# A four-layer block stack in fp32: two multiplications of the weights' fp4 rounding on GpSimd, another end for filler matmuls, and other due times

## The chip, the cores and the metric

The kernel runs on one core of a Trainium2 chip. The metric is the device time of one execution in microseconds (us); the time of a kernel is the median of several executions. Times of single instructions and waits are from one profiled execution.

## The reference, cut to what matters

The input x is 8 sequences of 1024 rows of 256 numbers (fp32). Four blocks follow, each added to what went in:

```python
x = x + attn0(layernorm(x))   # linear attention with running sums, then an inner FFN with GELU
x = x + ffn0(layernorm(x))    # relu(x @ w1 + b1) @ w2 + b2, 256 -> 1024 -> 256
x = x + attn1(layernorm(x))   # softmax attention, one head of 256
x = x + ffn1(layernorm(x))    # the FFN with fp4 rounding, 256 -> 704 -> 256
```

The change touches the rounding in the last block. It works on blocks of 16 numbers:

```python
def fp4_quant_dequant(x):
    xb = x.reshape(shape[:-1] + (shape[-1] // BLOCK, BLOCK))
    scale = jnp.max(jnp.abs(xb), axis=-1, keepdims=True) / 6.0
    scale = jnp.maximum(scale, jnp.float32(1e-12))
    xn = xb / scale
    idx = jnp.searchsorted(_MID, jnp.abs(xn))
    q = _GRID[idx] * jnp.sign(xn) * scale
    return q.reshape(shape)
```

Both sides of each product are rounded: the rows, for every row, and the weights w_gate, w_up (704 x 256) and w_down (256 x 704), once.

## The kernel before, in words

**Work.** The 8192 rows are cut into 64 chunks of 128 rows; four chunks are a group, two groups a sequence, so there are 16 groups. A group passes through the linear attention (linear_group, linear_span, linear_chunk), through the two dense FFNs (dense, with norms_1 after the first and norms_2 after the second), and then each chunk through the softmax attention and the fp4 FFN (soft_chunk). Different groups are in different stages at the same time, so that the stages share TensorE. A matmul of fp32 is two passes in the trace.

**Order.** Each stage is a Python generator that yields what its next instruction needs: an engine, tiles that must be written, free PSUM banks, a condition, a due time. Plan.run (L375) holds a small reckoning of when each engine and tile is free (Plan.took, L221) and always goes on with the part that can start soonest; among equals it prefers TensorE, and then the earliest due time. The instructions of each engine are pinned in the order in which they were issued: this order is fixed when the program is built, and the chip follows it. The queues of VectorE (DVE), ScalarE (ACT), GpSimd (POOL), TensorE (PE) and SyncE (SP, which issues the DMAs) are each in order.

**Due times.** T (L31) has a value for each kind of step, and EARLY (L78) other values for stages of the planner's time: below 130, 260, 400 and 2150, and after that. A value with a digit (lin2, weights0) is for one group alone. Other values are margins: ripe_* for how early something may be asked for, back and ahead for how far engines may run apart, shy for how much later ScalarE may be than VectorE and still get a layernorm's last step (layernorm, L705), gate0 and gate1 for the stage at which a group may begin.

**Fillers.** Where the planner finds that TensorE would wait over 1.6 us, it issues matmuls of the identity with itself into a free bank (fill, L1842); nobody reads these products. They run until 0.6 us ahead of the time at which the planner expects the next step.

**Transposes.** flip (L734) transposes a tile for the next product: on TensorE with a copy by ScalarE, if the planner finds no other step ready for TensorE, and otherwise by a copy on GpSimd (cut), a transposing DMA (spun) and a copy by ScalarE.

**The fp4 rounding** (fp4, L797) is a chain: VectorE takes the largest magnitude of each block (x_amax), the scale (x_s) and its reciprocal (x_r), multiplies the tile by x_r and a constant, ScalarE squares the scaled tile into q_c (bf16), VectorE rounds in two steps with q_c, and multiplies by x_s. fp4_weights (L838) runs the chain over 18 pieces of the three weights (tiles w_raw, at most 128 x 256), transposes each on TensorE, and copies it to wgT, wuT or wdT. When the last is done, "fp4" is added to the set weights. soft_chunk (L1688) runs the same chain over n (128 x 256) and hid (128 x 704) of each chunk, and asks for "fp4" in weights before the gate product (L1778).

All instructions are issued by one helper, so the profile has L422 for nearly all of them, and they are told apart by their tiles: half and hidden are the inputs of the two dense products with w_in and w_out, n2T and qT of the softmax scores, probT and vt of the attention product, xqT with wgT and wuT of gate and up, hqT with wdT of the last product, ident of fillers and of transposes.

Of the kernel before, what the change touches and what calls it, by code (L numbers as in the profile page):

```python
# [14 lines left out]
ALU = mybir.AluOpType  # L15
AX = mybir.AxisListType

P = 128
# [19 lines left out]
    gate1=1, by_act=1,  # L38
# [38 lines left out]

EARLY = [  # L78
    (130.0, dict(
        prods=0.359, pair=0.052, weighted=0.011, sums2=0.405, scores=0.861, turn_k=0.81,  # L80
        xo=0.296, step=0.131, dense=0.051, soft=2.551, soft1=0.323, soft2=0.706, fp4_over=5.754,
        weights=0.044, ripe_t=1.058, ripe_v=0.456, ripe_s=0.249, ripe_g=0.541, ripe_d=9.276,
        lin3=0.344, dense1=-0.003, weights0=-1.017, weights1=0.043,
    )),
    (260.0, dict(
        span=-0.064, prods=0.185, sums=-0.114, chunk=0.702, scores=0.785, dense=-0.085,
        soft=3.213, soft1=0.121, weights=-0.008, ripe_s=0.838, back=0.505, lin=-0.259,
        lin0=-0.325, norm0=-0.157, norm1=-0.26, weights0=-0.379, weights1=0.063, gate1=3.5,
    )),
    (400.0, dict(  # L90
        prods=-0.044, turn_k=0.82, turn_h=0.707, step=0.103, norm=0.746, soft=3.784, soft3=0.912,
        fp4=2.195, weights=0.078, ripe_d=7.2, ahead=0.839, lin2=-0.414,
    )),
    (2150.0, dict(
        prods=0.106, pair=0.211, sums=0.071, weighted=0.176, chunk=0.596, turn_k=0.801, xo=0.47,
        turn_h=0.706, soft3=1.013, fp4=3.733, fp4_over=6.383, weights=0.169, ripe_d=6.945,
        ahead=0.541, lin1=0.497, lin2=-0.186, lin3=-0.528, dense0=-0.017, dense1=0.151,
        norm0=-0.113, weights0=-0.286, gate1=3,
    )),
    (1000000000.0, dict(  # L100
        lin3=0.54, ripe_d=5.647, lin1=0.423, dense1=-0.052, scores=0.713, xo=0.287, chunk=0.609,
        shy=0.81, back=0.523, sums2=0.353,
    )),
]

# [18 lines left out]
class Plan:  # L124
# [206 lines left out]
    def dve(self, *tiles, **kw):  # L331
        return self.need("vector", tiles, **kw)
# [42 lines left out]
    def run(self):  # L375
        while self.parts:
            now = self.free.get("tensor", 0.0)
            best = None
            for part in self.parts:
                t = self.ready(part[1])  # L380
                if t is None:
                    continue
                stays = self.tiled and part[1].tiled
                queue = part[1].queue
                wait = max(max(t) - now - (0.3 if stays or part[2] < 0.0 else 0.0), 0.0)
                urgent = part[2] < 0.0
                unripe = 0.0 if urgent else max(t[1] + self.times[RIPE[queue]] - now, 0.0)
                key = wait, unripe, queue == "tensor", not stays, part[2]
                if best is None or key < best[0]:
                    best = key, part, max(t)  # L390
            assert best is not None, "every part waits for another"
            until = max(now, best[2])
            if until - self.ran > 1.6 and best[1][1].queue == "tensor" and self.fill is not None:
                if (self.banks_free(best[1][1].banks + 1) or 0.0) <= self.ran + 0.4:
                    self.fill(until - 0.6)
                    self.ran = until - 0.6
            if best[0][0] > 0.0 or best[1][1].queue == "tensor":
                self.free["tensor"] = max(now, best[2])
# [42 lines left out]
def block_stack_kernel(ctx: ExitStack, tc: tile.TileContext, a: dict, out: bass.AP):  # L441
# [20 lines left out]
    plan = Plan(tc, tc.nc)  # L462
# [328 lines left out]
    def blocks(t, width):  # L791
        return t[:, :width].rearrange("p (b e) -> p b e", e=QB)

    def wide(v, rows, nb):
        return v.unsqueeze(2).to_broadcast([rows, nb, QB])

    def fp4(src, width, rows=P, factor=1.0):  # L797

        nb = width // QB
        src = src[:rows, :width]
        amax = small([P, INTER // QB], "x_amax", 2)[:rows, :nb]
        nc.vector.tensor_reduce(
            amax, blocks(src, width), AX.X, ALU.max, apply_absolute_value=True  # L810
        )
        sc = small([P, INTER // QB], "x_s", 4)[:rows, :nb]
        nc.vector.tensor_scalar(sc, amax, factor / 6.0, 1e-12, ALU.mult, ALU.max)
        rc = small([P, INTER // QB], "x_r", 3)[:rows, :nb]
        nc.vector.reciprocal(rc, sc)
        yield dve(rc)
        nc.vector.scalar_tensor_tensor(
            blocks(src, width),
            blocks(src, width),
            -factor * (1.0 - 2.0**-23),  # L820
            wide(rc, rows, nb),
            ALU.mult,
            ALU.mult,
        )
# [12 lines left out]

    def fp4_weights():  # L838
        pieces = []
        for name, dstT in (("L1_ffn_w_gate", wgT), ("L1_ffn_w_up", wuT)):  # L840
            for r0, rows in INTER_TILES:
                turns = [(dstT[:, k, r0 : r0 + rows], k * P, P) for k in range(2)]
                pieces.append((a[name][r0 : r0 + rows, :], turns))
        for n in range(2):
            for c0 in range(0, INTER, D):
                width = min(D, INTER - c0)
                turns = []
                for f0 in range(0, width, P):
                    rows = min(P, width - f0)
                    dst = wdT[:rows, (c0 + f0) // P, n * P : (n + 1) * P]  # L850
                    turns.append((dst, f0, rows))
                pieces.append((a["L1_ffn_w_down"][n * P : (n + 1) * P, c0 : c0 + width], turns))
        raws = {}
        for i, (src, turns) in enumerate(pieces):
            for j in range(i, min(i + 3, len(pieces))):
                if j not in raws:
                    ahead = pieces[j][0]
                    raws[j] = (yield from fresh(
                        "soft",
                        dma(at=times["fp4"] + times["fp4_over"] * i / len(pieces), when=lambda: count["stage"] >= times["stage"]),  # L860
                        "w_raw",
                    ))[
                        : ahead.shape[0], : ahead.shape[1]
                    ]
# [823 lines left out]
    def soft_chunk(cc):  # L1688
# [209 lines left out]
```

## Time and profile before

| what | value |
|---|---|
| median of 3 runs | 2450.55 us (2448.66 to 2452.24) |
| the profiled execution's own time | 2450.4 us |
| its span | 2448.7 us |
| mean granted TensorE clock | 0.999 |
| DMA | 312.74 MB, 128 GB/s on average, 51% of the 16 engines' time |

The span is the time from the first to the last instruction of the profile, and the execution's own time has 1.7 us around it. Busy shares don't say how well an engine is used: matmuls overlap in the pipeline and their ends are modelled, so a busy TensorE may have slack, and fillers count as busy. A group's row has its line, engine, operation and tiles (out<-in), then the count, the busy time in us and the mean length of one in ns, and then the engine's idle time ahead of them and what ended it. A row of the timeline begins with start and length in us; what stands in brackets is idle time before it and what ended that.

### The profile page before, as it was taken

How to read it: one execution, taken by the hardware profiler on the slowest of the kernel's cores; microseconds unless marked ns; L12 is line 12 of the kernel's file. 1: busy time of each engine (PE TensorE's matmuls, PEld its weight loads, DVE VectorE, ACT ScalarE, POOL GpSimd, SP SyncE). 2: the span in 40 equal slices, each digit the busy share in tenths (PEclk: the TensorE clock that was granted, in tenths of full speed). 3: DMA queues.
4: the chain of work that ended last, by engine and by line, in shares of the span. 5: the costliest groups of instructions: out<-in, count | busy, mean ns of one | idle time of the engine just before them, and what ended most of it. 6: DMA issues, size and time to landing. Idle time of an engine off the chain costs nothing.

```text
span 2448.7 us, 47669 instructions
## 1 busy us (share of the span) xinstructions
PE 2419.4 (99%) x16473; PEld 1891.6 (77%) x16473; DVE 1914.3 (78%) x4152; ACT 1387.7 (57%) x2895; POOL 1276.9 (52%) x2258
## 2 busy tenths in 40 slices
PE   8999999999999999999999999999999999999999
PEld 6877777777877777777777777777777777887777
DVE  7778787878779787787877888688886978765887
ACT  5454556565565645656565565655556465555454
POOL 4354556565555656365563655546555474544342
PEclk9999999999999999999999999999999999999999
DMA  3355455564655555546555554556545555545332
GB/s 106 91 150 160 123 151 128 139 146 121 145 135 121 140 139 129 138 115 155 132 122 134 125 150 125 139 131 124 141 127 133 143 118 145 124 126 129 67 83 59
DMA packets 630897, 312.74 MB, mean 128 GB/s; under 512 B 434304, under 2 KB 619136, under 8 KB 630656
## 3 DMA queue, kind: packets, MB, share of 16 engines
q1 hardware_dynamic: 630656, 309.70, 51.3%
q8 instruction: 130, 2.13, 0.4%
q14 instruction: 111, 0.91, 0.1%
HBM read 188.17 MB, written 20.71 MB: 85 GB/s over the span
## 4 chain that ended last, share of the span: by engine, by line
PE 88%; DVE 6%; DMA 2%; POOL 2%; issue 1%; ACT 1%; SPq 0%; DVEq 0%; POOLq 0%; ACTq 0%
PE bank L422 88%; DMA spun<-cut 2%; DVE hid L422 1%; POOL cut L422 1%; DVE prod L422 1%; DVE ln_st L422 1%; DVE n L422 0%; POOL ln_rstd L422 0%; DVE sc L422 0%; DVE mx L422 0%; DVE res L422 0%; DVE u L422 0%; SPq L422 0%; POOL ln_shift L422 0%; DMA w_in<-in_L_attn_W_dram 0%
## 5 line engine op out<-in xcount | busy, mean ns | idle before, releaser
L422 PE MATMUL bank<-half,w_in 128*128 128x256 f32 x2048 | 529.2, 381 | 9.5 <-ACT half L422 6.4
L422 PE MATMUL bank<-w_out,hidden 128*128 128x256 f32 x2048 | 525.6, 383 | 1.5 <-DMA w_out<-in_L_attn_W_dram 1.4
L422 PEld LDWEIGHTS bank<-w_out,hidden 128*128 128x128 f32 x2048 | 377.4, 190 | 105.1 <-issue 45.7
L422 PEld LDWEIGHTS bank<-half,w_in 128*128 128x128 f32 x2048 | 384.5, 190 | 87.9 <-issue 22.4
L422 POOL TENSOR_SCALAR ln_ve<-ln_mv 128x1 f32<-128x1 f32 x384 | 107.1, 279 | 510.6 <-DVE ln_mv L422 489.4
L422 POOL TENSOR_TENSOR ln_rstd<-ln_ve,neghalf 128x1 f32<-128x1 f32 x384 | 251.3, 654 | 32.0
L422 ACT ACTIVATE hidden<-bank,c_L_ffn_b 128x256 f32<-128x256 f32 x256 | 120.8, 472 | 223.8 <-PE bank L422 222.0
L422 PE MATMUL bank<-n2T,qT 128*128 128x512 f32 x512 | 241.5, 594 | 0.0
L422 PE MATMUL bank<-vt,probT 128*128 128x256 f32 x1024 | 231.2, 379 | 0.0
L422 PEld LDWEIGHTS bank<-vt,probT 128*128 128x128 f32 x1024 | 194.2, 190 | 32.9 <-issue 6.9
L422 POOL COPY cut<-n 128x512 uint16<-128x512 uint16 x233 | 175.0, 757 | 79.8 <-DVE n L422 68.4
L422 ACT ACTIVATE hidden<-bank,c_L_attn_b 128x256 f32<-128x256 f32 x256 | 119.7, 469 | 170.8 <-PE bank L422 170.0
L422 POOL COPY cut<-prob 128x512 uint16<-128x512 uint16 x213 | 147.8, 716 | 92.0 <-ACT prob L422 50.4
L422 POOL COPY cut<-hid 128x512 uint16<-128x512 uint16 x172 | 116.4, 694 | 144.3 <-DVE rsum L422 66.3
L422 PE MATMUL bank<-wdT,hqT 128*128 128x256 f32 x768 | 175.9, 379 | 0.0
L422 PE MATMUL bank<-wgT,xqT 128*128 128x352 f32 x512 | 173.8, 462 | 0.5 <-ACT xqT L422 0.5
L422 PE MATMUL bank<-wuT,xqT 128*128 128x352 f32 x512 | 172.3, 459 | 0.0
L422 ACT COPY probT<-spun 128x512 uint16<-128x512 uint16 x250 | 159.6, 674 | 13.3 <-DMA spun<-cut 12.8
L422 PEld LDWEIGHTS bank<-wdT,hqT 128*128 128x128 f32 x768 | 145.6, 190 | 22.7 <-issue 1.9
L422 ACT ACT_TABLE_LOAD x124 | 159.1, 1283 | 4.4 <-PE bank L422 2.2
L422 PEld LDWEIGHTS bank<-n2T,qT 128*128 128x128 f32 x512 | 96.4, 190 | 69.7 <-issue 56.4
L422 PEld LDWEIGHTS bank<-wuT,xqT 128*128 128x128 f32 x512 | 97.3, 190 | 54.2
(272 smaller groups left out, 4831.1 us busy)
## 6 DMA issues: line engine op xcount, KB each, us to landing
w_in<-in_L_attn_W_dram SPq DMA_DIRECT2D x128, 256.0 KB
w_out<-in_L_attn_W_dram SPq DMA_DIRECT2D x128, 256.0 KB
w_in<-in_L_ffn_w_dram SPq DMA_DIRECT2D x128, 256.0 KB
w_out<-in_L_ffn_w_dram SPq DMA_DIRECT2D x128, 256.0 KB
spread<-packed SPq DMA_DIRECT2D x90, 256.0 KB
spun<-cut SPq DMA_TRANSPOSE x768
x<-in_L_attn_inputs_dram SPq DMA_DIRECT2D x64, 128.0 KB
xr<-in_L_attn_inputs_dram SPq DMA_DIRECT2D x64, 128.0 KB
```

The lines of the kernel that those rows point to most:

```text
L422: ins = method(*args, **kw)
```

## The change

Four things:

1. In fp4 a new argument, pooled, moves the two wide multiplications (by x_r with the constant, and by x_s) from VectorE to GpSimd. The constant is multiplied into x_r first, by one small instruction on VectorE. Only fp4_weights asks for it.
2. A burst of fillers ends 1.0 us ahead of the next step's expected time, and not 0.6.
3. soft_chunk waits for the weights' rounding before its second layernorm, and still before its gate product.
4. EARLY has other values in all its stages.

```diff
@@ EARLY
 (130.0, dict(
-        prods=0.359, pair=0.052, weighted=0.011, sums2=0.405, scores=0.861, turn_k=0.81,
-        xo=0.296, step=0.131, dense=0.051, soft=2.551, soft1=0.323, soft2=0.706, fp4_over=5.754,
-        weights=0.044, ripe_t=1.058, ripe_v=0.456, ripe_s=0.249, ripe_g=0.541, ripe_d=9.276,
-        lin3=0.344, dense1=-0.003, weights0=-1.017, weights1=0.043,
+        span=-0.169, prods=0.359, pair=0.034, weighted=0.011, sums2=0.405, scores=0.861,
+        turn_k=0.705, xo=0.464, turn_h=1.351, step=0.131, dense=0.051, norm=0.637, soft=2.551,
+        soft1=0.323, soft2=0.581, fp4=1.292, fp4_over=1.373, weights=0.044, shy=1.271,
+        ripe_t=1.087, ripe_v=0.344, ripe_s=0.249, ripe_g=0.541, lin0=0.017, lin2=-1.332,
+        lin3=0.34, dense1=-0.034, norm0=-0.179, weights0=-0.978, weights1=0.643,
     )),
...
     (2150.0, dict(
-        prods=0.106, pair=0.211, sums=0.071, weighted=0.176, chunk=0.596, turn_k=0.801, xo=0.47,
-        turn_h=0.706, soft3=1.013, fp4=3.733, fp4_over=6.383, weights=0.169, ripe_d=6.945,
-        ahead=0.541, lin1=0.497, lin2=-0.186, lin3=-0.528, dense0=-0.017, dense1=0.151,
-        norm0=-0.113, weights0=-0.286, gate1=3,
+        prods=0.106, pair=0.277, sums=-0.139, weighted=0.176, chunk=0.596, turn_k=0.859, xo=0.47,
+        turn_h=0.706, soft3=1.013, fp4=3.733, fp4_over=6.383, ahead=0.541, lin2=0.062,
+        lin3=0.238, dense0=-0.017, dense1=0.351, norm0=-0.113, norm1=-0.217, weights0=-0.402,
+        gate1=3, weights=0.1,
     )),
...
@@ Plan.run
-                    self.fill(until - 0.6)
-                    self.ran = until - 0.6
+                    self.fill(until - 1.0)
+                    self.ran = until - 1.0
@@ fp4
-    def fp4(src, width, rows=P, factor=1.0):
+    def fp4(src, width, rows=P, factor=1.0, pooled=False):
...
         nc.vector.reciprocal(rc, sc)
-        yield dve(rc)
-        nc.vector.scalar_tensor_tensor(
-            blocks(src, width),
-            blocks(src, width),
-            -factor * (1.0 - 2.0**-23),
-            wide(rc, rows, nb),
-            ALU.mult,
-            ALU.mult,
-        )
+        if pooled:
+            nc.vector.tensor_scalar(rc, rc, -factor * (1.0 - 2.0**-23), None, ALU.mult)
+            yield plan.pool(rc)
+            nc.gpsimd.tensor_tensor(
+                blocks(src, width), blocks(src, width), wide(rc, rows, nb), ALU.mult
+            )
+        else:
+            yield dve(rc)
...
         nc.vector.scalar_tensor_tensor(src, c, k, src, ALU.add, ALU.subtract)
         plan.drop(tile_c)
-        nc.vector.tensor_tensor(
+        if pooled:
+            yield plan.pool(src)
+        (nc.gpsimd if pooled else nc.vector).tensor_tensor(
             blocks(src, width), blocks(src, width), wide(sc, rows, nb), ALU.mult
         )
@@ fp4_weights
-            yield from fp4(raw, width, rows)
+            yield from fp4(raw, width, rows, pooled=True)
@@ soft_chunk
         yield dve(rows)
+        yield dve(when=lambda: "fp4" in weights)
         n = yield from layernorm("soft", rows)
```

Since the order of all engines follows from the due times, the built program differs nearly everywhere in its order, though hardly in what it computes: VectorE has 4148 instructions instead of 4154, GpSimd 2293 instead of 2263, TensorE 8359 matmuls and weight loads instead of 8349.

More of the change, by code (lines that the diff above doesn't have):

```diff
@@ L84 @@
+        soft1=0.323, soft2=0.581, fp4=1.292, fp4_over=1.373, weights=0.044, shy=1.271,
+        ripe_t=1.087, ripe_v=0.344, ripe_s=0.249, ripe_g=0.541, lin0=0.017, lin2=-1.332,
+        lin3=0.34, dense1=-0.034, norm0=-0.179, weights0=-0.978, weights1=0.643,
     )),
     (260.0, dict(
-        span=-0.064, prods=0.185, sums=-0.114, chunk=0.702, scores=0.785, dense=-0.085,
-        soft=3.213, soft1=0.121, weights=-0.008, ripe_s=0.838, back=0.505, lin=-0.259,
-        lin0=-0.325, norm0=-0.157, norm1=-0.26, weights0=-0.379, weights1=0.063, gate1=3.5,
+        span=0.206, prods=0.185, sums=-0.114, chunk=0.75, scores=0.785, dense=-0.085, soft=2.917,
@@ L89 @@
+        soft1=0.121, soft2=1.012, soft3=0.802, fp4=1.6, fp4_over=1.861, weights=0.254,
+        ripe_s=0.807, ripe_g=0.295, ripe_d=6.404, lin=-0.238, lin0=-0.325, lin3=-0.136,
+        norm0=-0.157, norm1=-0.498, weights1=-0.069, shy=0.28,
     )),
     (400.0, dict(
-        prods=-0.044, turn_k=0.82, turn_h=0.707, step=0.103, norm=0.746, soft=3.784, soft3=0.912,
-        fp4=2.195, weights=0.078, ripe_d=7.2, ahead=0.839, lin2=-0.414,
+        prods=-0.044, weighted=0.483, turn_k=0.82, turn_h=0.707, step=0.103, norm=0.746,
@@ L93 @@
+        soft2=0.443, soft3=1.065, fp4=1.6, fp4_over=2.0, weights=-0.335, ripe_s=0.657,
+        ripe_d=7.2, ahead=0.839, lin=-0.054, lin0=-0.32, lin2=-0.414, dense1=-0.304,
+        norm0=-0.074, norm1=-0.125, weights0=-0.121, gate0=3,
     )),
     (2150.0, dict(
-        prods=0.106, pair=0.211, sums=0.071, weighted=0.176, chunk=0.596, turn_k=0.801, xo=0.47,
-        turn_h=0.706, soft3=1.013, fp4=3.733, fp4_over=6.383, weights=0.169, ripe_d=6.945,
-        ahead=0.541, lin1=0.497, lin2=-0.186, lin3=-0.528, dense0=-0.017, dense1=0.151,
@@ L98 @@
-        norm0=-0.113, weights0=-0.286, gate1=3,
+        prods=0.106, pair=0.277, sums=-0.139, weighted=0.176, chunk=0.596, turn_k=0.859, xo=0.47,
+        turn_h=0.706, soft3=1.013, fp4=3.733, fp4_over=6.383, ahead=0.541, lin2=0.062,
+        lin3=0.238, dense0=-0.017, dense1=0.351, norm0=-0.113, norm1=-0.217, weights0=-0.402,
+        gate1=3, weights=0.1,
     )),
     (1000000000.0, dict(
-        lin3=0.54, ripe_d=5.647, lin1=0.423, dense1=-0.052, scores=0.713, xo=0.287, chunk=0.609,
-        shy=0.81, back=0.523, sums2=0.353,
+        lin3=-0.292, ripe_d=5.647, lin1=0.423, dense1=0.111, ripe_g=0.48, xo=0.287, chunk=0.609,
@@ L103 @@
+        shy=1.949, back=0.523, sums2=0.353, prods=0.274, soft=4.117, ripe_s=0.0, sums=-0.155,
+        ahead=0.482, weights=0.091, fp4_over=2.929, lin2=-0.073, soft1=0.477,
     )),
@@ L815, in fp4 @@
         nc.vector.reciprocal(rc, sc)
-        yield dve(rc)
-        nc.vector.scalar_tensor_tensor(
-            blocks(src, width),
-            blocks(src, width),
-            -factor * (1.0 - 2.0**-23),
-            wide(rc, rows, nb),
-            ALU.mult,
-            ALU.mult,
-        )
+        if pooled:
[6 more added lines that the diff above has]
+            yield dve(rc)
+            nc.vector.scalar_tensor_tensor(
+                blocks(src, width),
+                blocks(src, width),
+                -factor * (1.0 - 2.0**-23),
+                wide(rc, rows, nb),
+                ALU.mult,
+                ALU.mult,
+            )
         tile_c = yield from fresh("q_c", act(src))
```

## The prediction

> **What bounds the kernel now.** I read the busy row first, then the chain of waits, then TensorE's groups, its timeline around the fillers, and at last the rows of the operations that move.
>
> ```profile
> PE 2419.4 (99%) x16473; PEld 1891.6 (77%) x16473; DVE 1914.3 (78%) x4152; ACT 1387.7 (57%) x2895; POOL 1276.9 (52%) x2258
> PE 88%; DVE 6%; DMA 2%; POOL 2%; issue 1%; ACT 1%; SPq 0%; DVEq 0%; POOLq 0%; ACTq 0%
> L422 PE MATMUL bank<-ident 128*128 128x128 f32 x282 | 35.5, 285 | 3.1 <-POOL ident masks.py:199 3.1
> ```
>
> TensorE is the bound: busy 99%, and 88% of the chain that ended last. Only 29 us of the 2448.7 are idle, but 282 passes write products that nobody reads (two passes for each filler matmul of the program, so 141 fillers). Starts of neighbouring filler passes lie 112 ns apart, so one filler takes 0.224 us and all take 31.6 us. What can be won is in idle time and fillers, some 60 us, and most of that is the start-up, where no work exists yet.
>
> ```profile
> 320.00:500.00 180.00, 179.62 (x1269) 141.12 (x1268) 142.97 (x315) 103.09 (x217) 100.68 (x175) 1.00 0.55 137
> 1081.00:1375.20 294.20, 293.32 (x1998) 229.13 (x1998) 234.25 (x499) 171.14 (x350) 162.87 (x284) 1.00 0.54 133
> 2415.00:2449.00 34.00, 28.45 (x154) 23.31 (x153) 23.21 (x40) 10.82 (x21) 4.76 (x6) 0.99 0.19 47
> ```
>
> These are busy sums of three stretches (length; then PE, PEld, DVE, ACT, POOL). In the long middle the work repeats every two groups, 294.2 us, with 0.9 us idle in each. From 320 to 2150 us TensorE waits 5.2 us in all: six times for half from ScalarE, 4.8 us together, once 0.4 us for a weight. The middle offers at most this; but if the new order makes a wait there, it is paid about six times. The rest is the first 320 us and the last 34.
>
> ```profile
> 61.08 4.41 PE L422 MATMUL bank<-ident 128*128 128x128 f32 x38
> 101.52 5.97 PE L422 MATMUL bank<-ident 128*128 128x128 f32 x52
> 108.01 0.44 PE L422 MATMUL bank<-ident,h 128*128 128x128 f32 x2 [0.52 <-DVE h L422]
> 213.11 1.13 PE L422 MATMUL bank<-half,w_in 128*128 128x256 f32 x4 [1.83 <-DMA w_in<-in_L_attn_W_dram]
> 2431.07 5.07 PE L422 MATMUL bank<-ident 128*128 128x128 f32 x44
> ```
>
> There are twelve bursts. In eight the next step started within 0.1 us of the last filler; at six of these its input had been written 0.38 to 1.45 us before the start (0.05 where nothing was in the way): the filler held it up. After four a hole followed (0.32 to 1.99 us).
>
> **Fillers, and the end of a burst at 1.0 instead of 0.6 us.** I count them in the order in which the two built programs list their instructions; no time is taken from the planner's own reckoning. 141 become 139, but not in the same places:
> - Up to the second transpose of h before the first dense stage (108.0 us), 98 become 82: 16 x 0.224 = -3.6 us. Of the holes (1.9 us before) the two large ones, 1.11 and 0.68, grow by 0.4 each; the bursts that overshot only stop overshooting. +0.7. **Sum -2.9**; ends -3.6 (no hole grows) and +1.5 (seven holes of a full 1.0).
> - From there to 320 us, 15 become 18: +0.7, and two holes grow by 0.4: **+1.5** (0 to +2). The weights at 203 to 213 us stay late: in the new order of SyncE, too, the next w_in stands behind the four spread transfers.
> - In the middle, where there were none, eight stand ahead of a w_out product: 1.8 us plus a hole of up to 1.0. **+2.3** (0, if they take the place of another wait, to +2.8).
> - At the end 28 become 31, in four bursts instead of two: +0.7. Each hole could be 1.0; the holes in this tail were 0.32 and 1.39, and I add 1.1. **+1.8** (0 to +3.6).
>
> A longer hole could let the clock fall. The row speaks first:
>
> ```profile
> 28.00:32.00 4.00, 2.00 (x22) 1.00 0.11 33
> 32.00:35.00 3.00, 0.98 (x4) 0.50 0.01 3
> 35.00:39.00 4.00, 3.54 (x6) 0.52 0.43 118
> ```
>
> (length, PE busy, granted clock, DMA.) The clock halved at 32 us after 4 us in which TensorE was half busy, and half of the 3.5 us of work at the lower clock, 1.7 us, was lost. The Trainium skill (TensorE: Matmul & The Clock Gate, What's actually happening) lets it fall after about 3.4 us of idleness; by that rule holes of 1.5 us cost nothing, by the row a thin stretch is enough and each new dip costs about 1.7 us. This dip stays in both, since the same steps stand there. I add no second one, and keep 1.7 us for the range.
>
> **Transposes on TensorE** (flip, when the planner finds TensorE idle): 113 matmuls become 125, each two passes of 109 ns. Ten more stand in the first 320 us, where half may lie in idle time (+1.1), six more in the middle, which has no idle time (+1.3), four fewer between 2150 and 2400 (-0.9). **+1.5** (0 to +2.6). The DMA transposes fall from 768 to 762, on a queue off the path.
>
> **The two wide multiplications.**
>
> ```profile
> L422 DVE SCALAR_TENSOR_TENSOR w_raw<-w_raw,x_r x18: 345/416/605, 47.0 to 297.5; 128x256 f32<-128x256 f32 x14, 64x256 f32<-64x256 f32 x2, 128x192 f32<-128x192 f32 x2
> L422 DVE TENSOR_TENSOR w_raw<-w_raw,x_s x18: 357/425/835, 58.5 to 311.7; 128x256 f32<-128x256 f32 x14, 64x256 f32<-64x256 f32 x2, 128x192 f32<-128x192 f32 x2
> L422 DVE TENSOR_SCALAR x_s<-x_amax 128x16 f32<-128x16 f32 x78 | 18.9, 242 | 2.7
> L422 POOL TENSOR_TENSOR res<-n,b_L_attn_bo 128x256 f32<-128x256 f32 x64 | 51.0, 801 | 6.8 <-ACT carry_w L422 4.0 <-DMA b_L_attn_bo<-in_L_attn_bo_dram 2.1 <-ACT ahead L422 0.7
> ```
>
> VectorE loses 18 x (416 + 425 ns) = 15.1 us and gains 18 small multiplications at 242 ns, 4.4 us: 10.8 us less between 45 and 320 us. GpSimd has no such form with a broadcast input; its additions of this shape take 748 to 1011 ns, and I take 801, since it too reads two tiles: 36 x 0.80 = 29 us more on a queue that was half busy. A piece's chain gets 2 x 0.80 - 0.84 + 0.24 = 1.0 us longer and crosses engines four times. This is hidden: by the summed work of TensorE the last transpose of w_raw stands at 257 us (253 before), and the first gate product at 297 in both, so 40 us of other work cover it. Without that cover it would cost some 4 us once.
>
> A rule speaks against this part. The Trainium skill (SBUF — State Buffer, Who interferes with whom) says that a VectorE instruction with two inputs in SBUF is shut out while a GpSimd instruction reads SBUF. By the rows alone VectorE gains the 10.8 us. By the rule it is blocked in some of the new 29 us: it is busy 79% of that stretch, and if half of that has two such inputs, 29 x 0.79 x 0.5 = 11 us are lost again, an estimate. The x_s row, with 835 ns at most against 357 at least, is of a kind that would do so. I take it that little reaches TensorE: in 45 to 320 us it waits only 1.2 us for VectorE openly, and ahead of the second h, which is VectorE's chain, there are 36 fillers where 34 stood. Queued behind a wide multiplication on GpSimd are the layernorm steps (ln_rstd) and the cuts, each up to 0.8 us later, and ScalarE's n waits for these. **+1.0** (-1.2, the open waits gone, to +3).
>
> **The wait for the weights moved ahead of the layernorm** in soft_chunk: the weights' transposes end at 257 us of TensorE's work and the first attention product, after which it stands, at 266. It holds nothing: **0**; were it late, only a chunk's layernorm on VectorE stands behind it.
>
> **Due times in the middle.** Six transposes on TensorE in each two groups before and after; table loads on ScalarE fall from 16 to 14 per two groups (2 x 1.28 us, ScalarE is 57% busy). No wait shows in an order: **0** (-4.8 to +4.8).
>
> **Sum:** -2.9 + 1.5 + 2.3 + 1.8 + 1.5 + 1.0 = +5.2. The profiled execution took 2450.4 us (span 2448.7 and 1.7 around it), within 0.2 of the median 2450.55. **Forecast 2456 us, slower by 0.2%.** All lower ends give 2441, all upper ends with a second dip some 2472.
>
> **Rivals.** (1) Faster: the six waits for half go. For: in the new order two gate and two up products (2.4 us) lie between the transpose of n and the dense product at the step of that kind. Then -4.8, with -3.6 at the start, -1.2 for VectorE, +1.8 middle burst, +0.7 tail, +0.5 transposes: -6.6, 2444 us. Against: these waits only moved in the order, and ScalarE has to copy a second chunk too. (2) No change: the start's gain and half of these waits (-2.4) pay for the rest, with no price on GpSimd and no larger holes at the end: +0.7, 2451 us. (3) Much slower: the new order makes one wait of 2 us in each two groups, at the run of six attention and gate steps with no dense product between: 6 x 2 = +12 on the forecast, 2468 us. Against: the planner places transposes as often as before. That the change does nothing is excluded: the 36 multiplications stand on GpSimd.
>
> **Numbers.** Forecast 0.44, (1) 0.30, (2) 0.13, (3) 0.13. The range 2440 to 2470 leaves out about 2 in 10; the forecast's own is 2452 to 2462. A difference under 0.2% (4.9 us) can't be told from none. Faster: 0.28 + 0.02 = 0.30. Slower: 0.36 of the forecast, 0.01 and 0.13 = 0.50. Within: 0.20.
>
> **What would show it.** Right: filler passes near 278; the transpose of the second h before 108.0 us; a burst near 520 us; more idle time after the last gate product; w_raw on GpSimd near 0.8 us. Wrong: no wait for half left in the middle (rival 1), or a new wait that returns every 294 us (rival 3); a second stretch at half clock; w_raw on GpSimd over 1.0 us with late layernorms.

## The result, and the profile after

The changed kernel takes **2463.08 us** (median of 6 runs, 2460.08 to 2464.39), the kernel before in the same session 2450.33 us. The ratio is **1.0046, 95% interval 1.0036 to 1.0057**: slower by some 11 us, where 2456 (slower) was forecast with a range of 2440 to 2470. The profiled execution took 2464.0 us with a span of 2462.3, 13.6 more than the span before.

The page of the changed kernel (busy time, chain of waits, and the row of the fillers with its count, busy time, mean length, and idle time ahead):

```profile
PE 2426.9 (99%) x16481; PEld 1892.4 (77%) x16481; DVE 1907.2 (77%) x4146; ACT 1366.3 (55%) x2862; POOL 1317.9 (54%) x2288
PE 84%; DVE 10%; ACT 2%; POOL 2%; DMA 1%; issue 1%; SPq 0%; DVEq 0%; POOLq 0%; ACTq 0%
L427 PE MATMUL bank<-ident 128*128 128x128 f32 x278 | 35.2, 284 | 3.1 <-POOL ident masks.py:199 3.1
```

TensorE's idle time (span less busy) rose from 29.3 to 35.4 us, 6.1 more. Its busy time rose by 7.5 though its products are the same and the filler passes fell by 4: part of it is 12 more transposing passes in the trace (185 for 173, 1.3 us at 109 ns). Most of the rest is time at half clock: TensorE was busy for 14.3 us in three stretches at half clock (10.24, 3.41 and 3.41 us long), and before for 4.3 us in one (6.83 us long). Half of the difference, 5.0 us, is an estimate of what this added. VectorE is less busy and GpSimd more, as intended, and the chain has more of VectorE.

The busy sums of four stretches of the changed kernel (length; PE, PEld, DVE, ACT, POOL, each with its count of instructions; granted clock; DMA share and GB/s):

```profile
320.00:500.00 180.00, 179.62 (x1226) 140.24 (x1225) 144.71 (x318) 102.62 (x220) 99.82 (x179) 1.00 0.56 141
500.00:620.00 120.00, 115.92 (x815) 88.87 (x814) 87.14 (x186) 69.31 (x131) 58.37 (x108) 1.00 0.50 124
1085.00:1379.20 294.20, 293.48 (x1998) 228.77 (x1997) 234.25 (x498) 168.81 (x345) 169.12 (x283) 1.00 0.54 133
2428.00:2462.30 34.30, 29.60 (x164) 24.45 (x162) 23.52 (x42) 11.38 (x22) 3.70 (x6) 1.00 0.22 54
```

In the early part, in one stretch of the middle and in the tail the idle time is about that of before; stretches of equal length do not show whether a period has become longer. The stretch that stands out is 500 to 620 us: TensorE is idle for 4.1 us there, where about the same work had 1.1 us of idle time in the kernel before:

```profile
490.00:610.00 120.00, 118.94 (x824) 92.23 (x823) 93.34 (x195) 72.69 (x140) 70.57 (x119) 1.00 0.57 135
```

Busy sums do not add up to a finish time, so I also compared progress. Each product of TensorE, without fillers and transposes, is given its spacing from the traces (112 ns for 128 columns, 216 for 256, 429 for 512; passes of 32 rows a quarter), and the table says how many us later than the kernel before a run has done so much of this work (the columns; 2290 us in all). All kernels of this study stand in it; runs of one order differ by up to 2 or 3 us.

| run | 110 | 200 | 450 | 600 | 1200 | 1800 | 2250 | end |
|---|---|---|---|---|---|---|---|---|
| changed kernel | 0.7 | 0.2 | 1.2 | 6.4 | 7.3 | 9.0 | 13.3 | 13.7 |
| burst_alone | 1.0 | 1.5 | 0.6 | 1.2 | 1.1 | 1.1 | 1.1 | 3.0 |
| pool_alone | 0.0 | 0.5 | -0.5 | -0.5 | -0.3 | -0.1 | -0.1 | 0.0 |
| due_alone | 11.8 | 17.5 | 35.1 | 34.2 | 38.7 | 39.7 | 41.4 | 42.8 |
| after_burst_06 | 1.8 | 5.4 | 6.4 | 11.1 | 12.1 | 13.0 | 14.9 | 16.0 |
| all_due_old | 1.7 | 10.8 | 15.8 | 16.4 | 27.6 | 29.9 | 32.0 | 32.2 |
| new_order_mults_on_vector | 1.8 | 3.5 | 4.4 | 9.8 | 11.2 | 12.7 | 17.3 | 17.7 |
| late_due_old | -0.3 | -0.5 | -0.5 | -1.8 | 2.0 | 11.9 | 12.3 | 13.5 |
| early_due_old | 2.7 | 9.8 | 12.9 | 17.2 | 18.0 | 20.6 | 25.2 | 25.6 |
| one_due_moved | 0.7 | 4.0 | 9.8 | 14.1 | 21.6 | 24.2 | 32.5 | 36.0 |
| one_function_before | -1.1 | -1.0 | -0.7 | -0.8 | -0.8 | -0.4 | -0.4 | -0.4 |
| one_function_after | -1.2 | -0.3 | 0.6 | 2.6 | 3.6 | 5.5 | 8.5 | 8.9 |
| start_filled | -0.3 | 0.4 | 1.4 | 1.9 | 1.8 | 1.9 | 2.5 | 3.9 |

For the changed kernel: about 1 us is lost in the first 450 us of work, 5.0 us at one place between 450 and 500 (542 to 599 us of its trace), a slow drift after that, and 4.3 us between 1800 and 2250.

TensorE's timeline in the changed kernel, at the bursts that the prediction spoke of (start and length in us; in brackets idle time and what ended it):

```profile
23.87 4.18 PE L427 MATMUL bank<-ident 128*128 128x128 f32 x36
30.96 0.48 PE L427 MATMUL bank<-ident,n 128*128 128x128 f32 x1 [2.91 <-ACT n L427]
...
99.06 8.20 PE L427 MATMUL bank<-ident 128*128 128x128 f32 x72
107.11 0.38 PE L427 MATMUL bank<-ident,h 128*128 128x128 f32 x2
...
114.37 0.86 PE L427 MATMUL bank<-prod,hsum 128*32 128x128 f32 x24 [1.48 <-DVE prod L427]
...
564.73 1.95 PE L427 MATMUL bank<-ident 128*128 128x128 f32 x16
```

The second h comes at 107.11 instead of 108.01 us, but TensorE then waits 1.48 us for prod. The hole at 28 us has grown to 2.91 us (0.95 before). The burst in the middle is there, at 564.7 us; it was expected near 520.

Rows of TensorE's waits in the changed kernel (us in all, times, longest):

```profile
PE bank L427 <- ACT half L427: 3.0, 4, 1.8
PE bank L427 <- DVE hid L427: 2.1, 5, 0.4
...
PE bank L427 <- DVE sc L427: 1.5, 5, 0.3
```

The same for half in the kernel before:

```profile
PE bank L422 <- ACT half L422: 6.4, 9, 0.9
```

There hid had 1.4 us in one wait, and sc was not there. So the large waits for half did leave the middle, and two smaller ones came in their place in each period, one for hid and one for sc.

The two multiplications on GpSimd in the changed kernel (count, busy time, mean ns, idle time ahead):

```profile
L427 POOL TENSOR_TENSOR w_raw<-w_raw,x_s 128x256 f32<-128x256 f32 (+2 forms) x18 | 14.1, 784 | 29.8 <-DVE w_raw L427 29.8
L427 POOL TENSOR_TENSOR w_raw<-w_raw,x_r 128x256 f32<-128x256 f32 (+2 forms) x18 | 12.4, 690 | 25.7 <-DVE x_r L427 18.0 <-issue 7.4
```

Their mean is 0.74 us, against the 0.80 taken.

### The profile page after: what moved, and what is told of

Same layout as the page of the kernel before. It is cut to its first block, busy times and chain, and to the rows that moved or that the text cites. A ratio compares the mean times of both kernels' runs of the same rounds, so it can differ in the third digit from the quotient of the medians.

```text
span 2462.3 us, 47584 instructions
## 1 busy us (share of the span) xinstructions
PE 2426.9 (99%) x16481; PEld 1892.4 (77%) x16481; DVE 1907.2 (77%) x4146; ACT 1366.3 (55%) x2862; POOL 1317.9 (54%) x2288
## 4 chain that ended last, share of the span: by engine, by line
PE 84%; DVE 10%; ACT 2%; POOL 2%; DMA 1%; issue 1%; SPq 0%; DVEq 0%; POOLq 0%; ACTq 0%
PE bank L427 84%; DVE prod L427 3%; DVE hid L427 2%; DVE spread L427 1%; DMA spun<-cut 1%; DVE ln_st L427 1%; DVE n L427 1%; ACT L427 1%; POOL ln_rstd L427 0%; DVE x_amax L427 0%; DVE ln_mv L427 0%; DVE u L427 0%; DVE q L427 0%; DVE res L427 0%; POOL cut L427 0%
## 5 line engine op out<-in xcount | busy, mean ns | idle before, releaser
L427 POOL TENSOR_SCALAR ln_ve<-ln_mv 128x1 f32<-128x1 f32 x384 | 119.1, 310 | 573.4 <-DVE ln_mv L427 550.2
L427 POOL TENSOR_TENSOR ln_rstd<-ln_ve,neghalf 128x1 f32<-128x1 f32 x384 | 238.1, 620 | 32.0
```

Of the source, the lines that this page charges most:

```text
L427: ins = method(*args, **kw)
```

## Experiments

### Each part alone

Three theories: the loss lies in the order of instructions that the new due times make (1), in the multiplications on GpSimd (2), or in the earlier end of the bursts and the clock (3). Four kernels, on one chip, where the kernel before took 2452.35 us.

**burst_alone.** The kernel before with the new end of bursts.

```diff
-                    self.fill(until - 0.6)
-                    self.ran = until - 0.6
+                    self.fill(until - 1.0)
+                    self.ran = until - 1.0
```

> The kernel before with bursts ending 1.0 us ahead; the order of everything but the fillers is that of before (121 fillers instead of 141). Theory 1 (the loss lies in the order that the new due times make): 2449 to 2452 us. Theory 2 (the loss lies in the multiplications on GpSimd): the same. Theory 3 (the earlier end of the bursts lets TensorE's clock fall more often or for longer): 2453 to 2456, with more than 7 us at half clock.

Measured: 2453.80 us, ratio 1.0006 (0.9999 to 1.0012). The order of all other instructions is that of before; only the fillers are 121 instead of 141. Twenty fillers less, 4.5 us at 0.224, won nothing: the start is 1.0 us late at 110 us of work. The bare time and the some 14 us at half clock of its trace are what theory 3 gave; but on this chip the kernel before took 2452.35 us, so the difference is 1.5 us, and its interval holds zero.

**after_burst_06.** The changed kernel with the old end of bursts (the same edit, reversed).

> The changed kernel with bursts ending 0.6 us ahead again; same order but for the fillers (159 instead of 139). Theories 1 and 2: 2462 to 2465, no nearer to before. Theory 3: 2457 to 2460, and less than 13 us at half clock.

Measured: 2462.91 us, ratio 1.0051 (1.0038 to 1.0063), the same as with 1.0, and 17.1 us at half clock as there. Theory 3 falls: of the 11 us the end of the bursts makes 1.5 by burst_alone, and by its interval at most 3.

**pool_alone.** The kernel before with the two multiplications issued to GpSimd, while the planner still books them on VectorE, so that the order stays.

```diff
+            booked(
+                "gpsimd", ("vector", "scalar_tensor_tensor"), "tensor_tensor",
+                blocks(src, width), blocks(src, width), wide(rc, rows, nb), ALU.mult,
+            )
...
+        booked(
+            "gpsimd" if pooled else "vector", ("vector", "tensor_tensor"), "tensor_tensor",
+            blocks(src, width), blocks(src, width), wide(sc, rows, nb), ALU.mult,
```

> The kernel before with the two wide multiplications of the weights on GpSimd, in the same place; the planner books them as VectorE's, so that no other instruction changes its place. Theory 1: 2449 to 2452. Theory 2: 2455 or more, with late layernorm steps on GpSimd between 45 and 320 us. Theory 3: as theory 1.

Measured: 2451.45 us, ratio 1.0001 (0.9993 to 1.0009). The engine of these multiplications is worth nothing by itself, within the 2 us of the interval. Theory 2 falls, in the order of before.

**due_alone.** The kernel before with the new EARLY and nothing else.

> The kernel before with the new due times alone (multiplications on VectorE, bursts at 0.6, no earlier wait). Theory 1: 2459 or more, with waits of TensorE in the middle that before doesn't have. Theory 2: 2449 to 2453. Theory 3: 2449 to 2453.

Measured: 2494.13 us, ratio 1.0172 (1.0158 to 1.0186): nearly four times the loss of the whole change. Its timeline shows what such a loss is made of:

```profile
105.79 0.30 PE L427 MATMUL bank<-ident,hid 128*128 128x128 f32 x1 [1.82 <-DVE hid L427]
116.19 0.41 PE L427 MATMUL bank<-ident,w_raw 128*128 128x128 f32 x2 [1.94 <-DVE w_raw L427]
121.72 2.07 PE L427 MATMUL bank<-half,w_in 128*128 128x256 f32 x4 [4.44 <-ACT half L427]
...
228.72 2.03 PE L427 MATMUL bank<-w_out,hidden 128*128 128x256 f32 x4 [3.96 <-DMA w_out<-in_L_attn_W_dram]
```

In each of these rows TensorE's queue holds a product whose input is late, in an order that is fixed once it is built. Theory 1 holds as far as the loss is in the order. But by the ratios the new due times cost 42 us without the rest of the change and 11 with it, so they cannot be bad in themselves.

### The other corner, and the engine in the new order

**all_due_old.** The changed kernel with all due times of before: the multiplications are planned on GpSimd, bursts end at 1.0, and the early wait is in.

```diff
     (130.0, dict(
-        span=-0.169, prods=0.359, pair=0.034, weighted=0.011, sums2=0.405, scores=0.861,
...
+        prods=0.359, pair=0.052, weighted=0.011, sums2=0.405, scores=0.861, turn_k=0.81,
...
```

> The changed kernel (multiplications on GpSimd and planned there, bursts to 1.0, early wait) with all due times of before. Theory 1, the loss lies in the order that the new due times make: 2449 to 2453 us, no loss. Theory 2, the loss lies in the multiplications on GpSimd: 2460 us. The third theory, that due times fit only one sequence of steps: 2456 us or more, though no due time is new.

Measured: 2482.65 us, ratio 1.0122 (1.0108 to 1.0136). Theory 1 is wrong as I had put it: the due times of before do not bring the time of before back. That is what the third theory forecast. In the built programs the burst end leaves the order as it is everywhere. The early wait leaves it in three of the four corners of this table, but not in all_due_old: without the wait its order is another one, which was not run. So that corner is the multiplications and the early wait together.

| | due times of before | new due times |
|---|---|---|
| multiplications planned on VectorE | before: 1 | due_alone: 1.0172 |
| multiplications planned on GpSimd | all_due_old: 1.0122 (with the early wait) | changed kernel: 1.0046 |

Each list does better with its own sequence than with the other's: with the other's it lies 1.2 to 1.7% above the kernel before. The timeline of all_due_old shows the same kinds of late inputs as due_alone:

```profile
214.68 2.04 PE L422 MATMUL bank<-w_out,hidden 128*128 128x256 f32 x4 [3.76 <-DMA w_out<-in_L_attn_W_dram]
...
279.82 2.07 PE L422 MATMUL bank<-half,w_in 128*128 128x256 f32 x4 [3.29 <-ACT half L422]
```

**new_order_mults_on_vector.** The order of the changed kernel on every engine, but the two multiplications issued to VectorE (booked as GpSimd's).

```diff
-            nc.gpsimd.tensor_tensor(
+            booked(
+                "vector", ("gpsimd", "tensor_tensor"), "tensor_tensor",
                 blocks(src, width), blocks(src, width), wide(rc, rows, nb), ALU.mult,
```

> The order of the changed kernel on every engine, but the two wide multiplications are issued to VectorE (as one multiplication with its constant and one plain, as before). If the order of the changed kernel needs GpSimd for these (the new due times alone lost 43 us, with GpSimd only 13): 2470 to 2494 us, lost between 60 and 320 us. If the order alone makes the difference and the engine is indifferent, as in the order of before: 2460 to 2465 us. If GpSimd costs something (theory 2): under 2460 us.

Measured: 2465.31 us, ratio 1.0051 (1.0038 to 1.0064); its interval overlaps that of the changed kernel. In the new order, too, the engine is indifferent. What moving the multiplications changes is the planner's reckoning, and through it the order of everything.

### Which stages of the list

**late_due_old** has the old values in the last two stages of the list (from 400 us of the planner's time), **early_due_old** in the first three; the rest is the changed kernel. The lines are from late_due_old; early_due_old takes back the other stages in the same way, from the edit shown for all_due_old on.

```diff
     (2150.0, dict(
-        prods=0.106, pair=0.277, sums=-0.139, weighted=0.176, chunk=0.596, turn_k=0.859, xo=0.47,
...
+        prods=0.106, pair=0.211, sums=0.071, weighted=0.176, chunk=0.596, turn_k=0.801, xo=0.47,
...
```

> The changed kernel with the due times of before in the last two of the five stages (from 400 us of the planner's time on; the first three stages keep the new ones). Theory 1a, the new values from 400 us on make the crunch at 540 to 600 us, the drift after it and the wait at 1960 us: nearly the whole loss goes, 2452 to 2456 us. Theory 1b, the early stages leave the groups of rows in another phase and the middle only shows it: the loss stays, 2460 us or more. Theory 2, the loss is GpSimd's: stays too, 2460 or more.

> The changed kernel with the due times of before in the first three of the five stages (up to 400 us of the planner's time), the new ones after that. Theory 1a: the loss stays, 2460 us or more. Theory 1b: it goes, 2450 to 2454 us. A third theory, that each list of values fits only the one sequence of steps that it was set with: a loss of any size at the seam, 2460 to 2480 us, without a place in common with the changed kernel.

Measured: late_due_old 2463.91 us, ratio 1.0046 (1.0033 to 1.0060); early_due_old 2474.88, 1.0088 (1.0075 to 1.0102). Neither 1a nor 1b: neither half of the list carries the loss. By the table above late_due_old leads the kernel before by 1.8 us at 600 us of work, the place of the crunch gone, and then loses 13.7 us between 600 and 1800, where the changed kernel loses 2.6. The loss moves; it does not go. What makes its 13.7 us was not followed further.

### A single due time moved by 0.05

**one_due_moved** is the kernel before with one number changed. Small moves of other values in the same stage (soft, fp4 or norm by 0.05) leave the order of the built program as it was; this one changes it.

```diff
-        prods=-0.044, turn_k=0.82, turn_h=0.707, step=0.103, norm=0.746, soft=3.784, soft3=0.912,
+        prods=-0.044, turn_k=0.87, turn_h=0.707, step=0.103, norm=0.746, soft=3.784, soft3=0.912,
```

> The kernel before with a single due time changed by 0.05 (turn_k 0.82 to 0.87 in the third stage); multiplications, bursts and waits as before. It has the same instructions in another order from the early part on. Theory 3, that nearly any new order of the planner loses some us by a slip somewhere, and that the list of before is the rare one that has none: 2455 to 2480 us, with the loss in one or two places. Rival, the loss needs the change's own large edits: 2449 to 2453 us, as before.

("Theory 3" is here the third theory in what was expected of all_due_old, not that of the bursts.) Measured: 2485.26 us, ratio 1.0141 (1.0126 to 1.0156), three times the loss of the change under study, though nothing was added. TensorE's largest waits in it, and the largest single one:

```profile
PE bank L422 <- DMA w_in<-in_L_attn_W_dram: 4.8, 3, 3.0
PE bank L422 <- ACT half L422: 3.5, 5, 1.3
PE bank L422 <- DMA w_out<-in_L_attn_W_dram: 3.4, 1, 3.4
```

```profile
324.06 1.88 PE L422 MATMUL bank<-n2T,qT 128*128 128x512 f32 x4
329.38 3.14 PE L422 MATMUL bank<-w_out,hidden 128*128 128x256 f32 x8 [3.44 <-DMA w_out<-in_L_attn_W_dram]
```

The table shows the loss in small steps over the whole length rather than in one or two places; that part of the expectation was wrong. The size says what matters: of the orders run here none is faster than that of before, and this one, a single nudge away, lies 1.4% above it. So a loss of 0.5% needs nothing that is special to the multiplications or to the new list, and the table of four corners does not prove that a list fits one sequence only. One nudge is one case; how other orders near this one do was not measured.

### What makes the crunch at 540 to 600 us

ScalarE's timeline in the changed kernel:

```profile
553.19 1.28 ACT L427 ACT_TABLE_LOAD   x1
554.49 0.69 ACT L427 ACTIVATE k<-bank,bqk 128x512 f32<-128x512 f32 x1
555.19 1.28 ACT L427 ACT_TABLE_LOAD   x1
...
556.59 0.46 ACT L427 ACTIVATE hidden<-bank,c_L_attn_b 128x256 f32<-128x256 f32 x1
557.07 1.28 ACT L427 ACT_TABLE_LOAD   x1
558.36 0.69 ACT L427 ACTIVATE q<-bank,bqk 128x512 f32<-128x512 f32 x1
559.07 1.28 ACT L427 ACT_TABLE_LOAD   x1
560.36 0.69 ACT L427 ACTIVATE prob<-bank,nmax 128x512 f32<-128x512 f32 x1
```

Sigmoid for k and q, GELU for hidden and Exp for prob take turns, and each turn loads a table for 1.28 us: nine loads begin within 20 us of 550.5 us (never seven in the kernel before), though the whole kernel has fewer (112 for 125). The fourth theory: this crowd makes the crunch. Two kernels, in their own orders, give ScalarE one function everywhere; hidden, prob and e then have other values.

```diff
+            one_set = [AF.Sigmoid if isinstance(x, type(AF.Exp)) and x in (AF.Gelu, AF.Exp) else x for x in args]
-            ins = method(*args, **kw)
+            ins = method(*one_set, **kw)
```

> The changed kernel in its own order, but ScalarE is given Sigmoid wherever it has Gelu or Exp, so that it never loads another table; everything else is issued as it was (the activations of hidden, prob and e are other functions then, so these values and the output differ). Theory 4, the crunch at 540 to 600 us comes from ScalarE, which loads a table of 1.28 us nine times in 20 us there: the 6 us lost there go, the waits for probT at 569 and 592 us and the burst at 565 us are gone or below 0.5 us, and the whole is 2455 to 2458 us. Rival, the order of transposes and DMAs makes the crunch: at least 4 of the 6 us stay, 2460 us or more.

> The kernel before with the same edit (Sigmoid for Gelu and Exp, no table loads; the computation differs in the same way), for what the table loads cost in an order that does not crowd them. Theory 4: little, since no 20 us of its trace have seven loads and TensorE has 30 us of idle time in all, most of it in the start: 2447 to 2450 us. If it gains as much as the changed kernel (5 us or more), the loads cost both alike and the crunch is not theirs.

Measured: one_function_after 2458.53 us, ratio to the kernel before 1.0032 (1.0020 to 1.0044); one_function_before 2450.23, 0.9997 (0.9988 to 1.0006). The same stretch of one_function_after:

```profile
500.00:620.00 120.00, 118.33 (x831) 92.08 (x830) 89.63 (x190) 56.83 (x123) 62.65 (x112) 1.00 0.52 130
```

Idle time falls from 4.1 to 1.7 us, the waits for probT are gone, and by the reckoning of the table 1.6 us are lost from 450 to 500 us of work instead of 5.0. So taking the loads away wins 3.4 of the 5.0 us. The rest is the burst of 16 passes (1.8 us), which stays in the program though hidden is now ready 1.1 us before it ends. The time lies a little above what theory 4 gave: the drift and the loss after 1800 us are not the loads'. In an order that does not crowd them, 123 loads less are worth nothing.

A crowd is not enough, though. In late_due_old eight loads begin within 20 us of 545.2 us, in the same part of the work, and TensorE has no idle time there:

```profile
500.00:620.00 120.00, 120.00 (x833) 94.10 (x832) 92.60 (x192) 74.86 (x143) 62.29 (x109) 1.00 0.56 136
```

In all_due_old ten loads begin within 20 us of 713.0 us, and it loses 5.7 us from 610 to 650 us of work. So a crowd costs where products wait behind it, as here those of probT; at which number of loads it begins to, these runs do not say.

### The clock in the start

In each of the thirteen traces so far the clock halves between 30 and 35 us. **start_filled** is the kernel before with more unread products in its holes there, outside the planner's books.

```diff
+EXTRA = {0: 3, 4: 2, 10: 5, 11: 4, 13: 1}
...
+                for _ in range(EXTRA.get(plan.calls, 0)):
+                    more = self.engine.matmul(bank, lhsT=ident, rhs=ident, start=True, stop=True)
```

> The kernel before with 15 more unread products (3, 2, 5, 4 and 1) in the five holes of TensorE between 28 and 36 us (0.95, 0.65, 1.29, 1.14 and 0.46 us long), each filling less than its hole; everything else as before. In all thirteen traces so far TensorE's clock halved near 32 us. Reading A, the clock halves after a window of 3.41 us in which TensorE had too little work (under about 1.3 us, passes of 32 rows counted as a quarter): with 3.4 us more work in this stretch no stretch at half clock begins between 28 and 40 us. Reading B, it halves there for another reason (the first wide passes, or one idle hole): it stays. For the time: if the two n2T products are on the path of the start, 1.7 us less (2448.7 us, ratio 0.9993); if the bursts ahead of h absorb it as they absorbed the other shifts of the start, no change by 2330 us and 110 us of the trace stands as before.

Measured: 2454.83 us, ratio 1.0010 (1.0001 to 1.0018). Its stretches (columns as above; the clock is the third number from the end):

```profile
28.00:32.00 4.00, 3.64 (x32) 3.35 (x31) 3.51 (x7) 3.71 (x9) 0.27 (x1) 1.00 0.23 66
32.00:36.00 4.00, 4.00 (x38) 3.16 (x37) 3.53 (x9) 0.96 (x4) 2.56 (x4) 1.00 0.12 35
36.00:40.00 4.00, 3.61 (x16) 2.04 (x15) 3.08 (x8) 2.70 (x6) 0.81 (x2) 1.00 0.38 93
```

The clock stays at 1.00, where the prediction's fence for the kernel before had 0.50. Reading A holds, with one limit: the added products also shorten the holes, so this run does not tell the work of a window from the length of a hole (the last section does). The first n2T product starts 2.1 us later than in the kernel before (37.67 for 35.54 us) and the second 0.5 us later (39.49 for 38.97), so 1.6 us are won, near the 1.7 estimated. Before the added products its trace has a stretch at half clock that the kernel before does not have, at 16.7 us, and is late from there on; three other traces have one near 17 us, too. Nothing is left of the gain at the end. Why the whole is 0.1% slower I cannot say from one trace.

No kernel of the study is faster than the kernel before, so there is no version that beats both to show.

## Why the prediction was right, and where it was not

The sign and the range were right; the sum was +5.2 where the spans differ by 13.6, the medians by 12.7, and the ratio gives 11.3. The time lies above the 2452 to 2462 of the forecast's own. In part this is luck: the place in the middle that the prediction named makes 5 us of the loss, but 6.9 us come from a term that it put at 0, and 3.6 from fillers that were to win time and did not. Two of its signs of being wrong came (the large waits for half gone, more stretches at half clock), while rival 3, whose 2468 lies as near, did not: no wait of 2 us returns. By its steps:

- **Fillers up to the second h, -2.9: wrong.** The count was right (98 to 82) and h came 0.9 us earlier, but at 110 us of work the kernel is 0.7 us late. The failed step is "16 x 0.224 = -3.6": these fillers pass the time until VectorE has h and prod, so leaving them out makes idle time. burst_alone shows it without any other change: 20 fillers less, nothing won. That VectorE's chain keeps the time there is argued from the waits for h and prod, not shown by a run. The holes were priced too low as well: the one at 28 us was given 0.4 more, but it is 1.0 us in the mean of six traces whose bursts end at 0.6 (0.47 to 1.45) and 2.3 in the mean of the seven where they end at 1.0 (1.37 to 2.91; start_filled, which fills it, is left out).
- **From there to 320 us, +1.5: a little high.** 0.5 us from 110 to 450 us of work.
- **The burst in the middle, +2.3: right place, half the size.** 5.0 us are lost there. The burst was counted as the cause; it marks a place where ScalarE is late, and taking the loads of tables away wins 3.4 of the 5.0. I had counted table loads per two groups (fewer, so harmless) and not where they stand.
- **Due times in the middle, 0 (-4.8 to +4.8): mis-sized, and outside its bounds.** From 600 to 2250 us of work 6.9 us are lost. Rival 1's sign came true (the large waits for half went), but not its price: waits for hid and sc took their place. By the starts of the passes they cost 0.58 and 0.56 us in each period, where half had cost 0.93 to 1.07. A period, from one wait to the next of its kind, is 294.6 us long (904.33, 1198.89 and 1493.48 us) where it was 294.1 (1081.69 and 1375.77): 2.8 us in this stretch, of which the waits make a part and the rest is open. Two waits for hqT, at 1665 and 1961.5 us, cost 0.7 and 1.5 us by the starts, and the half clock after the second at most 1.7.
- **The tail, +1.8: too high.** 0.4 us, from 2250 to the end.
- **Transposes, +1.5: near by luck.** The trace has one pass for each transposing matmul, not two: 12 passes more, at most 1.3 us. The prediction's working, with half of the ten early ones in idle time, gives 0.75 us with one pass each.
- **The multiplications, +1.0 (-1.2 to +3): small, as said.** pool_alone gives 0.2 us, with an interval of about 2 us to either side. The rule of the Trainium skill (SBUF — State Buffer, Who interferes with whom) that spoke for 11 us of blocked VectorE time does not show at that size here: the other 451 VectorE instructions that start between 45 and 320 us took 220.0 us in sum before and 1.5 us more in pool_alone.
- **The early wait, 0: right.** The changed kernel's built program has the same order without it.
- **No second fall of the clock: wrong.** There are two more, at 139.9 and 1962.6 us, 3.41 us each and at most 1.7 us lost in each; and the first, the dip that was to stay as it is, lasts 10.24 us and not 6.83. The range held them.

What the prediction did not see at all is why the sum was small. It priced the parts as if the order around them stood still. Moving the multiplications in the planner, with the early wait, costs 1.2%, the new list alone 1.7%, and together they cost 0.5%: the re-set due times win back some 19 of the 30 us that the moved multiplications cost under the old ones. Whether a list exists that wins all of it back was not tried.

## What to carry to other kernels

Where a planner makes the order, price a moved operation in two steps: the engine with the order held (here nothing), and the new order that its booking makes (here, with the early wait, 30 us before the due times were set again, 11 after). A list of tuned values may do worse with any other sequence; compare with a kernel that has one value nudged before you put a loss down to the edit. Unread products that wait for another engine are not on the path, so fewer of them win nothing; and table loads are counted where they crowd ahead of something that is waited for, not over the whole.

## What the runs showed of the hardware

**The clock falls after a thin window, not only after an idle one.** In each trace, all stretches at half clock after 20 us begin on one grid of 3.41 us (lengths 3.41, 6.83 and 10.24 us). In the changed kernel one begins at 1962.63, after this on TensorE, and with these sums of the window before it and of the stretch itself:

```profile
1958.02 1.88 PE L427 MATMUL bank<-n2T,qT 128*128 128x512 f32 x4
1959.83 0.50 PE L427 MATMUL bank<-q,kz 32*128 32x128 f32 x6
1961.54 1.10 PE L427 MATMUL bank<-q,kz 32*128 32x128 f32 x26 [1.21 <-ACT hqT L427]
1962.57 2.05 PE L427 MATMUL bank<-half,w_in 128*128 128x256 f32 x4
```

```profile
1959.22:1962.63 3.41, 2.20 (x35) 1.33 (x33) 1.76 (x6) 1.01 (x3) 1.72 (x5) 1.00 0.60 145
1962.63:1966.04 3.41, 3.41 (x7) 2.10 (x7) 2.07 (x6) 2.64 (x5) 2.00 (x5) 0.50 0.55 154
```

TensorE was busy for 2.20 of 3.41 us, and the longest hole was 1.2 us; yet the clock halved, and four passes of 256 columns took 2.05 us instead of the 1.03 that they take elsewhere. Another window of the same grid and trace had less busy time and a longer hole, 1.48 us, and the clock stayed:

```profile
112.61:116.02 3.41, 1.93 (x36) 1.38 (x31) 3.24 (x8) 0.47 (x1) 0.88 (x2) 1.00 0.23 77
116.02:119.43 3.41, 3.41 (x21) 2.90 (x19) 2.31 (x10) 3.06 (x5) 1.78 (x5) 1.00 0.28 82
```

The difference is in the kind of work: counted by the spacings of the table above, transposes and fillers included and passes of 32 rows as a quarter, the window at 1959 us held 1.27 us of work and that at 112.6 us 1.52. Over the fourteen traces, from 20 us on, windows at full clock with less than 1.28 us of such work were followed by half clock in 37 of 37 cases, those with 1.28 to 1.40 in 5 of 10, and those with more in none of 9909. With passes of 32 rows counted as full ones this split is lost: the windows followed by half clock then count up to 3.97 us. The Trainium skill (TensorE: Matmul & The Clock Gate, What's actually happening) has the free-running window of 3413 ns, which the grid agrees with, and an idle window as the condition; the traces show that a little over a third of a window's work is the limit here, and that a pass of 32 rows counts for about a quarter of a full one. start_filled is the one run made to test it, and it held.

**GpSimd does the broadcast multiplication somewhat faster than its additions of the same shape**: 0.62 us at the median in pool_alone and in the changed kernel, where its additions of b_L_attn_bo took 0.73 at the median (0.80 and 0.81 in the mean); VectorE took 0.42 at the median. With VectorE's own work in another order beside it, in the changed kernel, the mean was 0.74 and the longest 1.53 us.
